# Q and K of three token groups by seven block products instead of eight, and the sums of W1 and W2 on another queue

## The chip, the cores and the metric

The kernel runs on one core of one Trainium2 chip. The core has TensorE (matrix products, results in PSUM), VectorE and ScalarE (elementwise work, both read PSUM), GpSimd (elementwise work, SBUF only) and SyncE, which issues most of the transfers. Each engine takes its own instructions in order. PSUM has eight banks of 128 x 512 float32. The metric is the device time of one execution in microseconds; the lower the better. Given is the median of three runs.

## The reference

One transformer block with conditioning, in float32, for 2 rows of 2048 tokens of width 512, 16 heads of 32, hidden width 2048:

```python
mod = silu(condition) @ Wada + bada              # 6 parts of width 512 for each row
sh_a, sc_a, gt_a, sh_m, sc_m, gt_m = split(mod, 6, axis=1)
xn = layernorm(x, g1, be1)
xm = xn * (1 + sc_a) + sh_a
x = x + gt_a * attention(xm, Wqkv, Wproj, bproj)  # causal, softmax over keys
xn = layernorm(x, g2, be2)
xm = xn * (1 + sc_m) + sh_m
h = gelu(xm @ W1 + b1)
x = x + gt_m * (h @ W2 + b2)
```

## The kernel before

For each of the two rows the kernel runs a Q, K, V stage (`Qkv.run`), an attention stage (`attention_phase`) and a projection (`project_phase`); after the second row comes a feed-forward stage for all tokens.

**The Q, K, V stage** takes the row's tokens in four groups g of 512 (`MT`). A group has 12 units n: eight for Q and K, in the order Q and K of output chunk f = 0, then of f = 1 to 3 (a chunk is 128 outputs, four heads), and four for V, one for each 128 tokens. A unit of Q or K is four products of a 128 x 128 block of `Wqkv` with 512 normalized, transposed tokens (`xmT`), added up in one PSUM bank (`ps_qk`, tag "mm", six banks in turn). A float32 product is two TensorE instructions. ScalarE then copies the bank to the first half of a tile `hl`, rounded to float32r (L860), VectorE subtracts that from the bank for the second half (L861), and SyncE stores the tile (L866). There are four `hl` tiles. This pair of ScalarE and VectorE steps is called the split below.

**Hooks.** After unit n, `between(n)` runs what belongs to other things: loads of the next tokens, their statistics, their normalization (n = 5, 8), their transposes through PSUM and the modulation that writes the next `xmT` (n = 6, 9; half of it by VectorE at L286, half by ScalarE at L291, unless `by_act`). It also calls `also(g, n)`, see below. After each product, `among(n, k)` may add attention scores of the same row: one score (`Row.score`, `Row.bank`) is a product of 128 queries with up to 512 keys into one of two banks with the tag "s", of which VectorE takes the maximum of each row (L484, or L479 where the causal mask cuts in). The number of scores at each place is worked out when the program is written, so that in group 1 the first of the attention units (4 heads by 512 queries) is scored and in groups 2 and 3 the next two. The keys and queries for that are loaded back from memory by SyncE (L339, L348) after chunk 0 of the group is stored.

**Sums of W1 and W2.** The feed-forward stage multiplies blocks two by two by the Strassen-Winograd scheme, with seven products and not eight; it needs sums of the blocks of W1 and W2, which are prepared during the Q, K, V stages. `Quarters` does this in 16 parts: `load` brings four blocks (L955, four transfers of 128 KB), `make` forms four sums on GpSimd (L967) and stores the seven blocks (L970, 896 KB). `FirstLayer` does a second level for W1 in the Q, K, V stage of row 1 (L997, L992, L1021). All of these transfers are issued by GpSimd. `also` calls them at fixed units; with at = 12 g + n, row 0 has 13 of the 16 parts, one each four units until at = 29 (`free`) and one each two units after that.

**Order.** Instructions wrapped in `act` or `mm` keep their program order on their engine; the others are ordered by a planner when the program is built, by its own model of time. Waits between engines are put in from the data that each instruction reads and writes.

**Memory reused.** `vv` holds the values of the row's 16 token tiles; tiles of tag "x" hold incoming tokens; four tiles "qst" hold the queries of attention units; `bgate` and `fold` are used in attention and projection.

Of the kernel before, what the change touches and what calls it, by code (L numbers as in the profile page):

```python
# [8 lines left out]
F32 = mybir.dt.float32  # L9
# [8 lines left out]
P = 128  # L18
# [9 lines left out]
def dit_block_kernel(  # L28
# [765 lines left out]

    class Qkv:
# [35 lines left out]
        def norm(self, g, j):  # L831

            b = self.row.b
            if j == 0:
# [3 lines left out]
                self.xmT[g][:, :, j * 2 * P : (j + 1) * 2 * P],  # L838
            )

        def group(self, g, hp, between, among):
# [5 lines left out]
            n = 0  # L847
            for f in range(C):
                for which in range(2):
                    ps = psum.tile([P, MT], F32, tag="mm", name="ps_qk")  # L850
                    w0 = which * D + f * P
                    for k in range(C):
                        mm(
                            ps, w[:, k, w0 : w0 + P], xmT[:, k, :],
                            start=(k == 0), stop=(k == C - 1),
                        )
                        among(n, k)
                    hl = hp.tile([P, 2, MT], F32R, tag="hl", name="hl", bufs=4)
                    scale = HD**-0.5 if which == 0 else 1.0
                    nc.scalar.activation(hl[:, 0, :], ps, AF.Copy, scale=scale)  # L860
                    nc.vector.scalar_tensor_tensor(  # L861
                        hl[:, 1, :], ps, scale, hl[:, 0, :].bitcast(F32),
                        ALU.mult, ALU.subtract,
                    )
                    dst = (qd if which == 0 else kd)[b][f]
                    nc.sync.dma_start(  # L866
                        dst[:, :, tok].rearrange("l p t -> p l t"), hl.bitcast(F32)
                    )
                    between(n)
                    n += 1  # L870
                if f == 0:
                    row.load_keys(0, g)
                    row.load_queries(g)
            for t in range(MTT):
# [9 lines left out]
                n += 1  # L884

        def run(self, hp, also):

            row = self.row
            for g in range(NG):

                def between(n):
                    if g + 1 < NG:
# [8 lines left out]
                        if n == 9 and g + 2 < NG:  # L901
                            self.load_x(g + 2)
                    elif n == 8:

                        row.rows(0)
                        act(nc.scalar.activation(first, eps, AF.Exp))
# [27 lines left out]
    class Quarters:  # L934
# [6 lines left out]
        def __init__(self):  # L941
            self.at, self.loaded = 0, []
# [1026 lines left out]
```

## Time and profile before

| | |
|---|---|
| median of 3 runs | 2307.22 us (2301.46 to 2310.62) |
| the profiled execution | 2301.71 us, its span on the core 2300.0 us |
| granted TensorE clock, mean | 0.999 |
| Q, K, V stage of row 0, groups 0 to 3 | 44.7, 47.6, 54.8, 49.7 us |
| Q, K, V stage of row 1, groups 0 to 3 | 43.0, 45.5, 51.9, 49.6 us |

The times of the groups are the lengths between the first products of Q and K of each, taken from the timeline of TensorE. In the rows of the profile, "PE" is TensorE's products, "PEld" its weight loads, "DVE" VectorE, "ACT" ScalarE, "POOL" GpSimd, "SP" SyncE. A row names the line of the kernel, the operation and "out<-in" by the names of the tiles; "<-" behind an idle time names who ended it. L204 is the helper through which every matrix product goes, so products are told apart by their tiles. The end of a matrix product is modelled and takes in the way through the array: products that follow each other overlap in their rows, and their pace is read from the starts.

### The profile page before, as it was taken

What the parts mean: (1) busy time and instruction counts of PE and PEld (TensorE: products, weight loads), DVE (VectorE), ACT (ScalarE), POOL (GpSimd) and SP (SyncE); (2) the same over time, 40 slices, a digit from 0 to 9 for tenths busy, and PEclk for the clock granted to TensorE, in tenths of its full rate; (3) what the DMA queues carried; (4) which work ended last, traced back from release to release, by engine and by line L of the source; (5) the groups of instructions that cost most, each with busy time, mean ns of one, the idle gap of its engine ahead of it and who ended that gap; (6) DMA issues with size and microseconds to landing.
All of it is one profiled execution on the core that took longest, in us unless ns stands there. A gap on an engine that the chain in (4) does not pass through costs nothing. (4 is left out here: it accounts for less than half of the span.)

```text
span 2300.0 us, 33469 instructions
## 1 busy us (share of the span) xinstructions
PE 2257.8 (98%) x12141; PEld 1384.9 (60%) x12141; DVE 1547.8 (67%) x3088; ACT 946.0 (41%) x1808; POOL 1291.1 (56%) x1036
## 2 busy tenths in 40 slices
PE   8999999999999999999999999999999999999998
PEld 3455455555554445554455545446888888888887
DVE  3366776777765525677677777555896876877787
ACT  2222555555556122155555555632332242252230
POOL 3335887878884543248788787553764602602510
PEclk9999999999999999999999999999999999999999
DMA  9867405151142799651421404265375654654643
GB/s 311 273 199 238 108 24 122 46 120 47 37 149 96 245 315 333 234 133 29 102 60 38 111 24 134 86 224 198 121 268 209 208 176 158 201 183 150 211 146 115
DMA packets 118525, 355.60 MB, mean 155 GB/s; under 512 B 14497, under 2 KB 15053, under 8 KB 103641
## 3 DMA queue, kind: packets, MB, share of 16 engines
q1 hardware_dynamic: 107040, 293.64, 42.0%
q0 software_dynamic: 10944, 59.28, 7.2%
q8 instruction: 96, 1.57, 0.3%
q14 instruction: 69, 0.56, 0.1%
q10 hardware_dynamic: 376, 0.55, 0.1%
HBM read 253.80 MB, written 107.48 MB: 157 GB/s over the span
## 5 line engine op out<-in xcount | busy, mean ns | idle before, releaser
L619 ACT ACTIVATE e<-st 128x512 f32<-128x512 f32 (+1 forms) x1152 | 573.4, 579 | 396.4 <-PE st L204 353.7
L484 DVE TENSOR_REDUCE mx<-s 128x1 f32<-128x512 f32 x612 | 413.3, 687 | 190.6 <-PE s L204 189.4
L649 POOL TENSOR_TENSOR ee<-ee,e 128x1024 f32<-128x1024 f32 x212 | 498.5, 2382 | 7.7 <-ACT e L619 7.7
L204 PE MATMUL s<-kst,qst 128*128 128x512 f32 (+3 forms) x1032 | 473.2, 460 | 11.9 <-DVE mx L484 5.8
L204 PE MATMUL st<-qst,kst 128*128 128x512 f32 (+3 forms) x1280 | 400.9, 378 | 0.0
L204 PE MATMUL ps_a<-sum,room 128*128 128x256 f32 x1504 | 356.8, 381 | 4.5 <-DVE c L1452 1.5
L204 PEld LDWEIGHTS ps_a<-sum,room 128*128 128x128 f32 x1504 | 281.2, 190 | 54.3 <-issue 6.0
L204 PE MATMUL o<-e,vv 128*32 128x512 f32 (+3 forms) x2560 | 300.8, 538 | 0.9 <-POOL e L628 0.9
L479 DVE CUSTOM_DVE_ANT_0 junk<-s,causal 128x128 bf16<-128x128 f32 (+3 forms) x420 | 206.0, 491 | 120.8 <-PE s L204 112.9
L204 PEld LDWEIGHTS s<-kst,qst 128*128 128x128 f32 x1032 | 193.9, 188 | 143.2 <-issue 65.1
L204 PEld LDWEIGHTS st<-qst,kst 128*128 128x128 f32 x1280 | 229.0, 188 | 68.2 <-issue 39.1
L649 POOL TENSOR_TENSOR ee<-e 128x1024 f32<-128x1024 f32 x84 | 198.2, 2382 | 118.6 <-ACT e L619 118.5
L204 PE MATMUL ps_qk<-xmT,wqkv 128*128 128x512 f32 x512 | 240.7, 598 | 1.8 <-DVE xmT L286 1.8
L628 POOL TENSOR_SCALAR_AFFINE_SELECT e<-e 128x256 f32<-128x256 f32 x256 | 103.7, 435 | 131.4 <-ACT e L619 129.4
L204 PEld LDWEIGHTS ps_qk<-xmT,wqkv 128*128 128x128 f32 x512 | 94.5, 191 | 98.4 <-issue 91.5
L1680 POOL TENSOR_TENSOR c<-c,h 128x512 f32<-128x512 f32 x40 | 58.6, 1484 | 159.1 <-ACT c L1678 159.1
L204 PEld LDWEIGHTS <-sel 32*128 32x128 bf16 x1152 | 29.7, 91 | 192.0 <-issue 189.9
L204 PE MATMUL ps_b<-sum,room 128*128 128x256 f32 x608 | 143.6, 379 | 0.0
L204 PEld LDWEIGHTS ps_b<-sum,room 128*128 128x128 f32 x608 | 115.0, 190 | 15.4
L204 PE MATMUL ps_v<-wqkv,xmT 128*128 128x512 f32 x256 | 122.1, 594 | 0.0
L204 PE MATMUL st<-fold,sel 32*128 32x512 bf16 (+1 forms) x1152 | 117.9, 372 | 4.3 <-DVE mhl L505 2.8
L204 PEld LDWEIGHTS o<-e,vv 128*32 128x32 f32 x2560 | 61.5, 108 | 98.7 <-issue 80.2
(182 smaller groups left out, 2945.8 us busy)
## 6 DMA issues: line engine op xcount, KB each, us to landing
qst<-q SPq DMA_DIRECT2D x128, 256.0 KB
room<-w1e SPq DMA_DIRECT2D x28, 1024.0 KB
kst<-k SPq DMA_DIRECT2D x24, 1024.0 KB
room<-w1e SPq DMA_DIRECT2D x28, 768.0 KB
room<-w2e SPq DMA_DIRECT2D x21, 1024.0 KB
q<-hl SPq DMA_DIRECT2D x32, 512.0 KB
k<-hl SPq DMA_DIRECT2D x32, 512.0 KB
room<-w2e SPq DMA_DIRECT2D x21, 768.0 KB
```

What stands on the lines that cost most here:

```text
L204: return tc.keep_in_program_order(nc.tensor.matmul(*args, **kw))
L479: nc.vector.tensor_tensor_reduce(junk[:, :w], s[:, :w], causal[:, QB - w :], 1.0, MASKED, ALU.add, ALU.max, m,)
L484: nc.vector.tensor_reduce(m, s[:, :w], axis=AX.X, op=ALU.max)
L619: act(nc.scalar.activation(e[:, h % 2, :w], sts[h][:, :w], AF.Exp))
L628: nc.gpsimd.affine_select(d, d, pattern=[[0, 2], [1, P]], compare_op=ALU.is_ge, fill=0.0, base=0, channel_multiplier=-1,)
L649: act(engine.tensor_tensor(dst, x, y, ALU.add))
L1680: nc.gpsimd.tensor_tensor(c, c, piece_of(base, i, t, pair), ALU.add)
```

## The change

Group 0 of each row stays as it was. In groups 1 to 3, Q and K go by pairs of output chunks (f = 0, 1 and f = 2, 3). For one pair, the outputs are split in two chunks, the 512 inputs in two halves and the 512 tokens in two halves, and the 2 x 2 by 2 x 2 block product is formed by seven block products (`sevens`). A block product is two matmuls of 128 x 128 weights with 256 tokens. Q and K of a pair run as two sets in turn: one product for Q, one for K, and so on. A set uses two PSUM banks, w and u, one for each output chunk; partial results are copied out by ScalarE to `kept` tiles (three a set) and added back by VectorE (three sums a set). Then each bank goes through the same split as before (`keep`).

The sums that this needs are formed by GpSimd: three new weight blocks for each set and one in place, after units 4 and 8 of group 0 (`weight_sums`), kept in an unused "qst" tile, `fold` and `bgate` (`scratch`); and four token blocks for each coming group at unit 10 (`token_sums`), kept in parts of `vv` that aren't filled yet, one new tile and tiles of tag "x". A group now begins with two units of V, then come the two pairs (units 2 to 5 and 6 to 9), then two units of V. Keys and queries are loaded after the first pair, not after chunk 0. The first "qst" tile is scratch, so the load of the fourth unit's queries waits until group 3 has used the weight sums in it.

The modulation of all groups but the very first is now wholly ScalarE's (`by_act`).

The transfers of `Quarters` and `FirstLayer` are issued by SyncE, and the store is a step of its own, called later than the sums. In row 0 the loads come at at = 11, 15, ..., 27, then 29, 31, ..., 43, the sums one unit after, the stores one unit after the sums (two where the loads come each two units); in row 1 `FirstLayer` loads at 11, 15, 22, 26, 35, 39, 43, sums two units later and stores four later.

```diff
@@ Qkv.norm
+                by_act=b > 0 or g > 0,
@@ Qkv.group
+            if g == 0:
...
+            n, half = 2 * C, MTT // 2
+            for t in range(half):
+                values(t, t)
+            for pair in range(C // 2):
+                self.sevens(g, pair, half + pair * C, keep, between, among)
+                if pair == 0:
+                    asked()
+            for t in range(half, MTT):
+                values(t, n + t)
+        def weight_sums(self, which, pair):
+            a = self.blocks(which, pair)
+            s1, s2, s4 = self.s[which, pair]
+            for d, x, y, op in (
+                (s1, a(1, 0), a(1, 1), ALU.add),
+                (s2, s1, a(0, 0), ALU.subtract),
+                (s4, a(0, 1), s2, ALU.subtract),
+                (a(1, 0), a(0, 0), a(1, 0), ALU.subtract),
+            ):
+                act(nc.gpsimd.tensor_tensor(d, x, y, op))
...
+            for d, u, v in (
+                (t1, x(0, 1), x(0, 0)),
+                (t2, x(1, 1), t1),
+                (t3, x(1, 1), x(0, 1)),
+                (t4, x(1, 0), t2),
+            ):
+                act(nc.gpsimd.tensor_tensor(d, u, v, ALU.subtract))
+        def sevens(self, g, pair, n, keep, between, among):
...
+            w = [self.psum.tile([P, MT], F32, tag="mm", name="ps_w") for _ in both]
+            u = [self.psum.tile([P, MT], F32, tag="mm", name="ps_u") for _ in both]
+            def product(ps, m, v, new=False):
+                for kk in range(2):
+                    mm(
+                        ps, m[:, kk, :], v[:, kk, :],
+                        start=new and kk == 0, stop=kk == 1, skip_group_check=not new,
+                    )
+                at = len(done)
+                done.append(n + at * 8 // 7 // 4)
+                among(done[-1], at * 8 // 7 % 4)
...
+            for q in both:
+                then = product(u[q][:, lo], a[q](0, 0), x(0, 0), True)
+                copy(kept[q][0], u[q][:, lo])
+                then()
+            for q in both:
+                then = product(w[q][:, hi], s[q][0], t1, True)
+                copy(kept[q][1], w[q][:, hi])
+                then()
+            for q in both:
+                then = product(u[q][:, lo], s[q][1], t2)
+                copy(kept[q][2], u[q][:, lo])
+                then()
+            for q in both:
+                then = product(w[q][:, hi], s[q][2], x(1, 1))
+                total(w[q][:, hi], w[q][:, hi], kept[q][2])
+                then()
+            for q in both:
+                then = product(u[q][:, lo], a[q](1, 0), t3)
+                total(u[q][:, hi], u[q][:, lo], kept[q][1])
+                then()
+            for q in both:
+                then = product(w[q][:, lo], a[q](0, 1), x(1, 0))
+                total(w[q][:, lo], w[q][:, lo], kept[q][0])
+                keep(w[q], q, 2 * pair)
+                then()
+            for q in both:
+                then = product(u[q][:, lo], a[q](1, 1), t4)
+                keep(u[q], q, 2 * pair + 1)
+                then()
@@ Qkv.run, between(n)
+                        if g == 0 and n == 4:
+                            self.scratch()
+                        if g == 0 and n in (4, 8):
+                            for which in range(2):
+                                self.weight_sums(which, n // 8)
+                        if n == 10:
+                            self.token_sums(g + 1)
@@ Quarters.load, .make, .store
-                act(nc.gpsimd.dma_start(w[:, n], src))
+                act(nc.sync.dma_start(w[:, n], src))
...
+        def store(self):
+            f, w = self.made.pop(0)
             dst = (w1d if f < FC // 2 else w2d)[:, :, :, f % (FC // 2), :]
             act(
-                nc.gpsimd.dma_start(
+                nc.sync.dma_start(
@@ row 0, also(g, n)
-            if 9 <= at < free:
-                if at % 4 == 1:
+            if 11 <= at <= free:
+                if at % 4 == 3:
                     quarters.load(room[0])
-                elif at % 4 == 3:
+                elif at % 4 == 0:
                     quarters.make()
-            elif at >= free and at % 2 == 1:
+                elif at % 4 == 1 and quarters.made:
+                    quarters.store()
+            if at >= free:
...
+                if at % 2 == 1 and quarters.at < early:
                     quarters.load(room[quarters.at % 2])
+                elif at % 2 == 0:
+                    if quarters.made:
+                        quarters.store()
+                    if quarters.loaded:
+                        quarters.make()
```

158 lines of the change are left out of this document (111 added, 47 removed).

## The prediction

> **What bounds the kernel now.** I read the page first: the engine shares, then the costliest groups.
>
> ```profile
> PE 2257.8 (98%) x12141; PEld 1384.9 (60%) x12141; DVE 1547.8 (67%) x3088; ACT 946.0 (41%) x1808; POOL 1291.1 (56%) x1036
> ...
> L204 PE MATMUL ps_a<-sum,room 128*128 128x256 f32 x1504 | 356.8, 381 | 4.5 <-DVE c L1452 1.5
> L204 PEld LDWEIGHTS ps_a<-sum,room 128*128 128x128 f32 x1504 | 281.2, 190 | 54.3 <-issue 6.0
> ...
> L204 PE MATMUL ps_qk<-xmT,wqkv 128*128 128x512 f32 x512 | 240.7, 598 | 1.8 <-DVE xmT L286 1.8
> ```
>
> TensorE is busy 98% of the span, and before its 512 instructions for Q and K it stood idle 1.8 us in all. So work taken off TensorE there is time, until another engine binds. A share is a mean, so next comes the table of busy times over the stretches of the three later token groups of row 0 and of row 1. Its columns are the stretch, its length, then busy time of TensorE, weight loads, VectorE, ScalarE and GpSimd, the granted clock, the DMA share and GB/s.
>
> ```profile
> 65.10:112.70 47.60, 47.60 (x146) 22.66 (x145) 20.06 (x61) 13.62 (x26) 13.41 (x18) 1.00 0.93 296
> 112.70:167.50 54.80, 54.16 (x178) 28.01 (x177) 34.35 (x90) 12.98 (x25) 21.22 (x31) 1.00 0.68 205
> 167.50:217.20 49.70, 49.70 (x141) 24.78 (x140) 30.32 (x64) 8.38 (x14) 24.92 (x37) 1.00 0.80 243
> ...
> 842.20:887.70 45.50, 45.50 (x129) 22.31 (x128) 19.58 (x59) 12.92 (x25) 18.32 (x18) 1.00 1.01 352
> 887.70:939.60 51.90, 51.26 (x155) 26.82 (x154) 33.00 (x85) 13.11 (x26) 23.89 (x23) 1.00 0.99 349
> 939.60:989.20 49.60, 49.60 (x137) 24.73 (x135) 30.29 (x64) 8.37 (x14) 0.00 (x0) 1.00 0.45 138
> ```
>
> TensorE fills each stretch at full clock. But VectorE is at 61 to 64% in groups 2 and 3 (30.32 of 49.70): they carry the attention scores beside Q and K. And the DMA engines are at 0.68 to 1.01 in all but the last. These are the two covers that the change leans on.
>
> **The change on TensorE.** One matmul of the program is two instructions here. Their spacing is read from unbroken runs in the timeline (start, duration, count); a row's own duration holds the drain too and can't be used.
>
> ```profile
> 799.25 24.20 PE L204 MATMUL ps_qk<-xmT,wqkv 128*128 128x512 f32 x56
> 823.29 1.04 PE L212 MATMUL ps_xt<-ident,x 128*128 128x128 f32 x8
> ...
> 2004.93 1.89 PE L204 MATMUL ps_b<-xm,room 128*128 128x256 f32 x8
> ...
> 2013.57 0.81 PE L204 MATMUL ps_a<-sum,room 128*128 128x256 f32 x3
> ```
>
> (823.29 - 799.25) / 56 = 0.429 us for 512 columns; (2013.57 - 2004.93) / 40 = 0.216 us for 256, in the feed-forward stage, which already multiplies by sevens. A pair (two output chunks of Q and of K) is 4 x 4 matmuls of 512 now, 32 instructions, 13.73 us; after, 2 sets x 7 products x 2 matmuls of 256, 56 instructions, 12.10 us. That is 1.63 us less; two pairs in three groups of two rows are 12 pairs: **19.6 us less**. The 24 added weight loads of a pair cost nothing of their own as long as each hides under a stream of 0.216.
>
> In the feed-forward rows it does: eight weight loads of 0.19 fit in each 1.73 us. If loads didn't overlap, a pair would go from 32 x 0.619 to 56 x 0.406 us, 2.9 longer, and the kernel to 2307 + 35 = 2342. The Trainium skill (TensorE: Matmul & The Clock Gate, "The mechanism") says that a weight load overlaps with matmuls in flight only where their row groups differ, which is that case, since all these use all rows; the spacing of 0.216 with 0.19 loads speaks against it here.
>
> **What waits inside a set of seven.** Each product needs the copy or sum made of its bank by ScalarE or VectorE before. With two sets in turn, three other products, 3 x 0.86 = 2.6 us, lie between. A copy or a sum takes about 0.4:
>
> ```profile
> L1452 DVE TENSOR_TENSOR c<-y,ps_a x40: 406/420/422, 1689.8 to 2281.7; 128x256 f32<-128x256 f32 x40
> L1768 ACT COPY c<-ps_a x16: 372/372/377, 1663.9 to 2221.3; 128x256 f32<-128x256 f32 x16
> ```
>
> In the feed-forward stage, with one set at a time, all 1504 instructions of the first group on the page waited 4.5 us together. I take 0 for this chain as such. ScalarE gains 72 copies of 0.372, and by_act moves 4 modulations each of seven group preparations to it; at 8 to 14 us of 45 to 55 it has room.
>
> **VectorE in groups 2 and 3** is the dear term. A set adds three sums of 0.42; 72 in all, 30 us; by_act takes off 28 modulations of 0.53, 15 us, but none in group 3, which prepares no next group. The rows of groups 2 and 3 of row 0, by shape:
>
> ```profile
> L484 DVE TENSOR_REDUCE mx<-s 128x1 f32<-128x512 f32 x48 | 33.0, 688 | 18.6 <-PE s L204 18.5
> L861 DVE SCALAR_TENSOR_TENSOR hl<-ps_qk,hl 128x512 fp32r<-128x512 f32 x16 | 11.0, 685 | 14.4 <-ACT hl L860 14.4
> ...
> L286 DVE TENSOR_SCALAR xmT<-ps_xt,a,c 128x256 f32<-128x256 f32 x4 | 2.0, 534 | 0.0
> ```
>
> The work isn't spread evenly: the splits (L861) of a pair all fall on its last four products. There VectorE has 2 sums of 0.42, 4 splits of 0.69 and 4 scores of about 0.65 (an estimate: two of three are the first row's 0.69, masked ones are shorter): 6.2 us. TensorE has 4 products of 0.864 and 4 scores of 0.21 ((49.70 - 48 x 0.858) / 41): 4.3 us. VectorE falls 1.9 us behind, and TensorE feels it through the two score banks:
>
> ```profile
> 955.22 0.69 DVE L484 TENSOR_REDUCE mx<-s 128x1 f32<-128x512 f32 x1 [0.40 <-PE s L204]
> 955.83 0.68 DVE L861 SCALAR_TENSOR_TENSOR hl<-ps_qk,hl 128x512 fp32r<-128x512 f32 x1
> ...
> 960.50 0.69 DVE L484 TENSOR_REDUCE mx<-s 128x1 f32<-128x512 f32 x1
> ```
>
> ```profile
> 959.66 0.80 PE L204 MATMUL s<-kst,qst 128*128 128x512 f32 x1
> ```
>
> The score started at 959.66 is reduced at 961.19, 1.53 us later, and its bank is wanted two products on, after 2.15: 0.6 us of slack. So 1.9 - 0.6 = 1.3 us of stall; rows that follow directly start 0.61 and not 0.69 apart, which over ten rows gives 0.8 back: 0.5. I take 1.0 for each of the 8 pairs of groups 2 and 3, since the split of a sum also has to wait for ScalarE's 0.60: **8 us more**. Ends: 0 (the scores order themselves around it), and 2.5 a pair, 20 us, if VectorE idles 0.6 before both splits that follow a sum. Group 1 has 16 scores on its 40 slots, not 40, and I take 0.
>
> **GpSimd** gains 32 weight sums of 0.74 and 24 token sums of 1.27 us, and loses its DMA issues:
>
> ```profile
> L992 POOL TENSOR_TENSOR w<-w 128x512 f32<-128x512 f32 x28 | 35.0, 1272 | 2.0 <-DMA w<-w1d 1.3
> L967 POOL TENSOR_TENSOR w<-w 128x256 f32<-128x256 f32 x12 | 8.5, 742 | 8.6 <-DMA w<-in_L_cond_W_dram 8.4
> L955 POOL DMA_DIRECT2D w<-in_L_cond_W_dram x12 | 6.4, 546 | 5.6 <-DMA w2d<-w 3.6 <-DMA w<-w1d 1.9
> ```
>
> At 13 to 25 us of 45 to 55 it has room. Token sums start at unit 10; the first is wanted after three units of V (10.3 us) and two products, 12 us later; modulation and sum take 3.5. Cost 0; without the cover the price is the 5.1 us of four sums a group.
>
> **SyncE** takes over the loads and stores of W1 and W2, in order with the stores of Q and K and the loads of keys and queries. What is queued behind a waiting load there is the store of a split, and behind that, with four hl tiles, ScalarE's next split. From unit 33 to 43 of row 0, six loads each wait for a store issued one unit before.
>
> ```profile
> L970 POOL DMA_DIRECT2D w1d<-w x8: 1067/1067/1109, 23.7 to 167.5; - x8
> ...
> DMA to landing us min/median/max: 5.4/5.8/11.3
> ```
>
> A cycle is landing 5.8, four issues of 0.55 and the store, 8.6 us, for two units of TensorE at (49.70 - 3.3 + 2) / 12 = 4.0 each, 8.1. SyncE falls 0.5 x 6 = 3 us behind; an hl tile is reused a pair, 15 us, later and needs 5.8 to land, so 9 are covered: cost 0. Already now the splits of units 6 and 7 of group 3, whose products end near 196 and 200 (units of 4.1 from 167.5), come at 206.32, and TensorE is busy all through that stretch, which supports the cover:
>
> ```profile
> 206.32 1.06 ACT L860 ACTIVATE hl<-ps_qk 128x512 fp32r<-128x512 f32 x2
> ```
>
> **The start.** GpSimd's first load of W1 now shares the DMA engines with the load that TensorE needs:
>
> ```profile
> 5.37 2.90 POOL L955 DMA_DIRECT2D w<-in_L_cond_W_dram  x4
> ...
> 14.97 1.72 PE L204 MATMUL ps_mod<-wada,sc 128*32 128x512 f32 x4 [0.23 <-DMA wada<-in_L_cond_Wada_dram]
> ```
>
> It goes to unit 11. 0.5 MB at about 300 GB/s is 1.7 us, the most that this can give; 0 the least. I take 0.8 less.
>
> **The sum.** -19.6 - 0.8 + 8.0 = -12.4 us. The profiled execution took 2301.7 us (span 2300.0) and is 5.5 under the median of three, so it would go to 2289; against the median of 2307.2 I predict **2295 us**.
>
> **Rivals.**
> 1. VectorE keeps up, no stall: 2307 - 21 = 2286. For it: it is 61 to 64% busy over a group. Against it: the four products above.
> 2. VectorE becomes the bound at every pair's end: with 2.5 us a pair the gain of groups 2 and 3 is gone, 2307 - 20.4 + 20 = 2307. For it: L861 already idles 14.4 us for ScalarE's half.
> 3. Slower: SyncE's queue. With stores landing in 11.3 us, as the slowest did, a cycle is 14.1, six cycles fall 36 us behind, 9 covered: a stall of 27 in row 0, 2307 - 12 + 27 = 2322. It eats the gain from a lag of 9 + 12 = 21 us on, that is landings over 8.8 us on average. For it: DMA shares near 1. Against it: the median of 5.8.
> 4. Weight loads that don't hide: 2342, as worked out above. Against it stand 1504 rows of this kernel.
>
> **How the numbers follow.** Forecast (stalls of 4 to 13 us, 2290 to 2299) 0.52, rival 1 0.15, rival 2 0.17, rival 3 0.15, rival 4 0.01. A change under 0.5%, 11.5 us, is about what measurement can't tell from none. Faster by more (under 2295.7): rival 1's 0.15 and somewhat over half of the forecast, 0.30, make 0.45; within: the other 0.22 of it and rival 2's 0.17, 0.39; slower: rivals 3 and 4, 0.16. The range for 8 in 10 runs from just under rival 1 to past rival 2 and into rival 3, 2284 to 2315.
>
> **What would show it.** Right: rows of 128x256 spaced 0.216 for Q and K; group 1 stretches down by 3.3 us (47.6 to 44.3), groups 2 and 3 by 1 to 1.5; TensorE's idle for VectorE before scores up from under 1 us to about 8; first Q product about 1 us earlier than 20.37. Wrong: stretches of groups 2 and 3 as long as before (rival 2), or ScalarE's splits waiting on stores of hl and TensorE idle behind them in units 38 to 48 of row 0 (rival 3), or Q and K rows spaced over 0.25 (rival 4).

## The result, and the profile after

The changed kernel takes 2318.4 us (median of six runs, 2315.4 to 2320.6); the kernel before took 2304.0 beside it (six runs). The ratio is 1.0059, with a 95% interval of 1.0042 to 1.0077: 10 to 18 us slower, where I had predicted 12 us faster. The profiled execution took 2319.8 us (span 2318.1).

The page of the changed kernel, engine shares and packets:

```profile
PE 2248.9 (97%) x12429; PEld 1443.0 (62%) x12429; DVE 1560.1 (67%) x3132; ACT 981.8 (42%) x1908; POOL 1279.0 (55%) x998
...
DMA packets 153858, 355.66 MB, mean 153 GB/s; under 512 B 14496, under 2 KB 56012, under 8 KB 138968
```

TensorE is 9 us less busy than before (2248.9 against 2257.8), though the kernel is longer: part of the gain shows even so, and waits have eaten it. The stretches of groups 1 to 3 of row 0, then of row 1, for the changed kernel. They run from the first product of a group's first pair to that of the next group's, so that each holds eight units of Q and K and four of V, as before. The one of group 3 is carried 6.9 us past the attention's first score, for the two units of V that this group now has ahead of its first pair: its length compares with the one before, but the busy times in its last 6.9 us are the attention's. Columns as in the prediction.

```profile
68.47:112.69 44.22, 44.22 (x193) 31.71 (x192) 21.93 (x68) 18.13 (x41) 7.21 (x11) 1.00 0.91 264
112.69:180.42 67.73, 53.53 (x226) 37.71 (x225) 37.25 (x100) 18.43 (x41) 25.33 (x30) 0.92 0.81 234
180.42:229.70 49.28, 47.12 (x202) 34.30 (x201) 38.69 (x89) 16.15 (x33) 14.97 (x23) 1.00 0.89 263
854.96:897.70 42.74, 42.40 (x177) 31.35 (x176) 20.91 (x67) 18.27 (x41) 15.01 (x12) 1.00 0.86 281
897.70:952.94 55.24, 51.19 (x203) 36.51 (x202) 36.50 (x95) 18.64 (x41) 18.23 (x15) 0.97 0.86 303
952.94:1002.30 49.36, 44.52 (x184) 32.23 (x183) 36.73 (x84) 13.36 (x27) 12.10 (x11) 1.00 0.80 268
```

Group 1 is shorter by 3.4 and 2.8 us (47.60 and 45.50 before), group 3 by 0.4 and 0.2. Group 2 is longer, by 12.9 us in row 0 (54.80 before) and 3.3 in row 1 (51.90). What TensorE waited for in the whole of the changed kernel, and then in the kernel before (total, times, longest):

```profile
PE s L204 <- DMA qst<-q: 11.5, 1, 11.5
PE s L204 <- DVE mx L484: 9.3, 12, 1.4
...
PE s L204 <- DVE mhl L505: 5.8, 11, 1.1
PE st L204 <- ACT e L619: 4.3, 2, 4.1
...
PE s L204 <- DVE mx L479: 2.9, 4, 1.5
```

```profile
PE s L204 <- DVE mx L484: 5.8, 10, 0.8
PE s L204 <- DVE mhl L505: 4.7, 10, 0.6
```

Two single waits are new. **In group 2 of row 0** TensorE stands 11.5 us before the first score of the third attention unit, because that unit's queries aren't there (for the first 1.5 us of this the score has to wait for VectorE anyway, whose last step for the unit before ends at 154.1). SyncE's queue from the end of the first pair on (start, duration, line, transfer):

```profile
130.67 0.37 SPq L861 DMA_DIRECT2D q<-hl  x1
131.22 0.62 SPq L1136 DMA_DIRECT2D w1d<-w  x1
134.49 0.37 SPq L861 DMA_DIRECT2D k<-hl  x1
135.09 0.77 SPq L861 DMA_DIRECT2D q<-hl  x1
137.98 1.94 SPq L1116 DMA_DIRECT2D w<-in_L_cond_W_dram  x4
140.02 0.41 SPq L861 DMA_DIRECT2D k<-hl  x1
140.48 0.48 SPq L339 DMA_DIRECT2D kst<-k  x1
145.25 0.53 SPq L1136 DMA_DIRECT2D w1d<-w  x1
145.87 3.85 SPq L1116 DMA_DIRECT2D w<-in_L_cond_W_dram  x4
149.76 1.42 SPq L339 DMA_DIRECT2D kst<-k  x3
151.22 2.70 SPq L348 DMA_DIRECT2D qst<-q  x4
```

The last K of the pair (VectorE ended its split at 135.66), the three later loads of keys and all loads of queries stand behind a load of W1 that waits for a store to land (137.98), a store that waits for GpSimd's sums (145.25) and the next load. The last load of queries is issued at 153.9. They land at about 164, as TensorE's row shows:

```profile
164.05 1.19 PE L204 MATMUL s<-kst,qst 128*128 128x512 f32 x2 [11.47 <-DMA qst<-q]
165.04 1.91 PE L204 MATMUL ps_v<-wqkv,xmT 128*128 128x512 f32 x2
```

Stretches of these microseconds, columns as above:

```profile
158.00:162.00 4.00, 0.00 (x0) 0.00 (x0) 0.00 (x0) 0.00 (x0) 0.00 (x0) 0.50 1.11 205
162.00:164.00 2.00, 0.00 (x0) 0.00 (x0) 0.00 (x0) 0.00 (x0) 0.00 (x0) 0.50 1.16 274
164.00:166.00 2.00, 1.95 (x5) 1.27 (x5) 1.15 (x2) 0.00 (x0) 0.81 (x2) 0.50 1.10 360
166.00:168.00 2.00, 2.00 (x6) 0.97 (x4) 0.44 (x3) 0.00 (x0) 1.92 (x3) 0.64 1.13 374
```

The DMA engines are full (share over 1) and move only 205 to 274 GB/s while TensorE waits. The clock granted to it fell to 0.50 at about 157.2 and was full again at about 167.4: 3.4 us of work at half the clock, so that the stall costs an estimated 1.7 us more than its length.

**At the start of row 1's attention** the exponentials wait for a store. Their tiles take the room of FirstLayer's tiles, whose last store is called at unit 47. SyncE, ScalarE and TensorE there:

```profile
994.64 0.33 SPq L1190 DMA_DIRECT2D w1e<-w  x1
...
1003.12 1.09 ACT L619 ACTIVATE e<-st 128x512 f32<-128x512 f32 x2 [4.78 <-DMA w1e<-w]
1003.76 1.07 PE L204 MATMUL st<-fold,sel 32*128 32x512 bf16 x2 [4.14 <-ACT e L619]
```

The granted clock is 0.50 from about 1003.7 to 1013.9, and the first product with the values comes 17.0 us after the first score, where it took 9.5 before.

The account by stages, after less before in us: first Q product -1.8, row 0's group 0 -1.7, groups 1 -6.1, groups 2 +16.3, groups 3 -0.7, the two attention starts +0.6 and +7.5, the rest of the attention +0.4, the feed-forward stage +3.5: together +18 of one profile against the other. Two of these terms aren't the change's. The feed-forward stage, from its first product with a tile `sum`, took 720.9 us before and 724.4 after, but 720.6 to 725.6 in the executions below, and 724.5 in one of the kernel before with one edit far from it. And the -1.7 in row 0's group 0 is the clock: the profile of the kernel before has 0.50 granted there from about 20.8 to 24.3 us, that of the changed kernel has 1.00 throughout. Of the other 16 runs with seven products, 9 have such a low clock there, with 51.6 us from the first Q product to the first pair, and 7 haven't, with 49.9. Without the two, +16 remains.

### The profile page after: what moved, and what is told of

It reads as the page before. It is cut to its first block, busy times and chain, and to the rows that moved or that the text cites. A ratio compares the mean times of both kernels' runs of the same rounds, so it can differ in the third digit from the quotient of the medians.

```text
span 2318.1 us, 34368 instructions
## 1 busy us (share of the span) xinstructions
PE 2248.9 (97%) x12429; PEld 1443.0 (62%) x12429; DVE 1560.1 (67%) x3132; ACT 981.8 (42%) x1908; POOL 1279.0 (55%) x998
## 2 busy tenths in 40 slices
DMA packets 153858, 355.66 MB, mean 153 GB/s; under 512 B 14496, under 2 KB 56012, under 8 KB 138968
## 5 line engine op out<-in xcount | busy, mean ns | idle before, releaser
L484 DVE TENSOR_REDUCE mx<-s 128x1 f32<-128x512 f32 x612 | 413.3, 687 | 225.3 <-PE s L204 223.8
L204 PE MATMUL s<-kst,qst 128*128 128x512 f32 (+3 forms) x1032 | 438.1, 427 | 30.6 <-DMA qst<-q 11.5
L628 POOL TENSOR_SCALAR_AFFINE_SELECT e<-e 128x256 f32<-128x256 f32 x256 | 104.4, 441 | 84.9 <-ACT e L619 51.9
L1128 POOL TENSOR_TENSOR w<-w 128x256 f32<-128x256 f32 x64 | 45.2, 729 | 142.0 <-DMA w<-in_L_cond_W_dram 130.2
L484 DVE TENSOR_REDUCE mx<-st 128x1 f32<-128x512 f32 x156 | 107.0, 686 | 3.8 <-PE st L204 1.3
```

The costliest lines, as they stand in the source:

```text
L204: return tc.keep_in_program_order(nc.tensor.matmul(*args, **kw))
L484: nc.vector.tensor_reduce(m, s[:, :w], axis=AX.X, op=ALU.max)
L628: nc.gpsimd.affine_select(d, d, pattern=[[0, 2], [1, P]], compare_op=ALU.is_ge, fill=0.0, base=0, channel_multiplier=-1,)
L1128: act(nc.gpsimd.tensor_tensor(w[:, n], w[:, x], w[:, y], op))
```

## The experiments

My theory (A) was that SyncE's queue makes the loss: the queries and keys of group 2 and the last store of FirstLayer. The rival (B) was that the seven products don't pay in groups 2 and 3, since VectorE binds. Ratios are to the kernel before, run beside each, with 95% intervals.

### The two halves apart

Seven products, with the transfers of W1 and W2 on GpSimd and called as in the kernel before:

```diff
-                act(nc.sync.dma_start(w[:, n], src))
+                act(nc.gpsimd.dma_start(w[:, n], src))
...
-            if 11 <= at <= free:
-                if at % 4 == 3:
+            if 9 <= at < free:
+                if at % 4 == 1:
                     quarters.load(room[0])
```

> The changed kernel with all transfers of Quarters and FirstLayer back on GpSimd and at the units of the kernel before; Q and K by seven products stay. Theory A (SyncE's queue made the loss: the queries of group 2 come 11.5 us late in row 0, and the last store of sums stands ahead of the attention of row 1 for 7.5 us): both stalls go, with them the low clock behind the first (some 2 us): 2318 - 11.5 - 2 - 7.5 = 2297, group 2 of row 0 down from 67.7 to about 54. Theory B (the sevens themselves don't pay in groups 2 and 3, since VectorE binds there): group 2 stays above 60 us, and the time stays at 2310 or over. What would speak for neither: TensorE waiting for the token sums, which now stand behind GpSimd's loads.

Eight products, with these transfers on SyncE and called as in the changed kernel:

```diff
-                act(nc.gpsimd.dma_start(w[:, n], src))
+                act(nc.sync.dma_start(w[:, n], src))
```

> The kernel before with only the transfers of Quarters and FirstLayer moved to SyncE, at the units of the changed kernel; Q and K by eight products, and keys and queries asked for after unit 1 of a group. Theory A: the queries of group 2 are asked for four units before the loads come each two units, so that stall is small, but the attention of row 1 still starts 7.5 us late: 2304 + 7.5 - 1.8 (start) = 2310, up to 2320 if the queries are late here too. Theory B: no loss from the queue, 2302 to 2304.

Both were wide of both theories: 1.0159 (1.0140 to 1.0178) and 1.0159 (1.0144 to 1.0174), some 37 us slower each, while both together cost 14. TensorE's waits with seven products and GpSimd's queue:

```profile
PE s L204 <- DMA qst<-q: 13.4, 2, 7.4
...
PE o L204 <- POOL e L628: 7.1, 3, 6.2
...
PE ps_w L204 <- POOL vv L959: 5.8, 2, 4.0
```

On GpSimd, loads that wait for a store to land stand ahead of the token sums that the sevens need (L959) and of the masks of the attention (L628). So, with the calls where the kernel before has them, that queue doesn't serve the sevens. With eight products and SyncE's queue, ScalarE and SyncE at the start of row 1's attention:

```profile
1007.32 12.01 SPq L1029 DMA_DIRECT2D w1e<-w  x2
```

```profile
1025.98 1.08 ACT L619 ACTIVATE e<-st 128x512 f32<-128x512 f32 x2 [13.01 <-DMA w1e<-w]
```

SyncE is so far behind that two stores of FirstLayer are left at 1007. The move to SyncE with the new call times, which I had priced at nothing, costs 37 us when done alone. First products with the values come 19.2 and 24.5 us after the first scores (8.9 and 9.5 before), and row 1's group 2 takes 60.6 us (51.9 before).

### Asked late, or queued?

In the changed kernel keys and queries are also asked for four units later. That alone, in the kernel before:

```diff
-                if f == 0:
+                if f == (0 if g == 0 else 2):
                     row.load_keys(0, g)
```

> The kernel before with one edit: keys and queries of groups 1 to 3 are asked for after unit 5 of their group, as in the changed kernel, and not after unit 1. All transfers of W1 and W2 stay on GpSimd. Theory A1 (the stall before the scores of group 2 comes of the late asking itself, four units later on DMA engines that are busy): TensorE waits 5 to 10 us before these scores, 2301 + 8 = 2309. Theory A2 (it comes of SyncE's queue, that is of the loads and stores that stand ahead there): under 2 us, 2301 to 2303.

1.0004 (0.9990 to 1.0018): no cost. SyncE's rows there, with group 2 starting at 114.27:

```profile
144.48 1.86 SPq L348 DMA_DIRECT2D qst<-q  x3
```

The last query load is issued 32 us after the pair's first product, and nothing waits. But this doesn't clear the late asking in the changed kernel: here VectorE ends the unit before only 46.3 us after that product, so that the queries are wanted later than there (41.4). The next run takes the loads of keys and queries out of SyncE's queue:

```diff
@@ Row.load_keys
-                nc.sync.dma_start(
+                (nc.gpsimd if c == 0 and g > 0 else nc.sync).dma_start(
@@ Row.load_queries
-                nc.sync.dma_start(
+                (nc.gpsimd if 0 < u < NQ else nc.sync).dma_start(
```

> The changed kernel with the loads of keys and queries of groups 1 to 3 issued by GpSimd in place of SyncE. Theory A: they no longer stand behind the loads and stores of W1 in SyncE's queue, and the 11.5 us that TensorE waits for queries in group 2 of row 0 go, with some 2 us of low clock: 2318 - 13 = 2305. Theory B (the keys and queries are late because the stores of Q and K land late, or because the DMA engines are full): the wait stays at 8 us or more, 2315 to 2318.

1.0028 (1.0019 to 1.0038), 2307.8 us. TensorE's wait in group 2 of row 0 falls from 11.5 to 2.2 us, the stretch is 56.4 us in place of 67.7. GpSimd's queue there, with the pair starting at 114.87, and TensorE:

```profile
141.24 1.09 POOL L348 DMA_DIRECT2D qst<-q  x2
142.32 2.18 POOL L339 DMA_DIRECT2D kst<-k  x4
144.50 1.09 POOL L348 DMA_DIRECT2D qst<-q  x2
```

```profile
156.51 0.70 PE L204 MATMUL s<-kst,qst 128*128 128x512 f32 x2 [2.22 <-DVE mhl L505]
```

VectorE's step L505 ends at 155.8 and the last query load lands at 156.3, so that 0.7 us of the 2.2 are still the queries'. The issue is 10.5 us earlier than in the changed kernel, and from its end to the score it's about 11 us here and 10 there: the DMA engines didn't get faster, the queue let go earlier. Theory A holds for this stall. Which of SyncE's work stands in the way? First the stores alone were taken off it, and called at the end of `make`:

```diff
             self.made.append((f, w))
+            self.store()
...
-                nc.sync.dma_start(
+                nc.gpsimd.dma_start(
                     dst.rearrange("p n c d -> p (n c) d"),
```

> The changed kernel, with the stores of the sums (Quarters and FirstLayer) issued by GpSimd right behind its sums; the loads stay on SyncE at the same units. Theory A1 (SyncE's queue is held by stores that wait for GpSimd's sums): the 11.5 us wait for the queries of group 2 shrinks to under 5, the last store of FirstLayer falls at unit 45 and not 47, so that the wait at the start of row 1's attention loses some 4 us: 2318 - 7 - 2 - 4 = 2305. Theory A2 (the queue is held by loads that wait for the store ahead of them to land, and by full DMA engines): the loads still wait, the queries still come 8 us or more late, 2314 to 2318.

1.0047 (1.0032 to 1.0061); the wait stays at 11.0 us, A2. Then row 0's loads were moved so that none comes at units 28 to 32, the later ones to 33, 35, ..., 43:

```diff
-            if 11 <= at <= free:
-                if at % 4 == 3:
-                    quarters.load(room[0])
+            if at in (8, 11, 14, 17, 20, 23, 26):
+                quarters.load(room[0])
...
-                if at % 2 == 1 and quarters.at < early:
+                if at % 2 == 1 and at >= 33 and quarters.at < early:
```

> The changed kernel with one edit: row 0's parts of W1 and W2 are loaded at units 8, 11, 14, 17, 20, 23, 26 and then 33, 35, ..., 43, so that SyncE's queue and the DMA engines have no loads of W1 between unit 28 and unit 33, where the keys and queries of group 2 are asked for. Theory B1 (the queries are late because loads of W1, ahead of them in the queue and beside them on full DMA engines, come in these units): the 11.5 us wait goes, with 2 us of low clock: 2318 - 13 = 2305. Theory B2 (they are late because VectorE finishes the splits of the first pair late and their stores take long to land, whatever else is loaded): the wait stays at 6 us or more, 2312 to 2318.

1.0118 (1.0102 to 1.0133), slower still, and no test of the pause: in group 1 the queue fell behind. Its loads of W1 there, with the same room each time:

```profile
78.67 2.50 SPq L1116 DMA_DIRECT2D w<-in_L_cond_W_dram  x4
91.05 2.03 SPq L1116 DMA_DIRECT2D w<-in_L_cond_W_dram  x4
104.44 4.21 SPq L1116 DMA_DIRECT2D w<-in_L_cond_W_dram  x4
123.66 1.91 SPq L1116 DMA_DIRECT2D w<-in_L_cond_W_dram  x4
```

```profile
132.42 2.08 PE L204 MATMUL ps_w<-vv,qst 128*128 128x256 f32 x4 [9.31 <-POOL vv L959]
```

One room goes round in 12 to 19 us: load, landing, sums, store, landing. GpSimd's weight sums wait for those loads, and the token sums wait behind them. The pause came again with group 1 left at its pace, and two parts moved to row 1:

```diff
-        free, early = 2 * (C * 2 + MTT) + 5, 13
+        free, early = 2 * (C * 2 + MTT) + 5, 11
-                if at % 2 == 1 and quarters.at < early:
+                if at % 2 == 1 and at >= 33 and quarters.at < early:
...
-            late_loads = (11, 15, 22, 26, 35, 39, 43)
+            late_loads = (11, 20, 24, 28, 32, 36, 40)
```

> The changed kernel with 11 parts in row 0 (loads at units 11, 15, 19, 23, 27, 33, 35, ..., 43) and five in row 1 (units 0, 1, 6, 7, 12), FirstLayer's loads then at 11, 20, 24, 28, 32, 36, 40. Group 1 keeps its pace of one part each four units, unlike the run with the pause, and no load of W1 is called at units 28 to 32. Theory B1 (loads of W1 ahead of the keys and queries and beside them): the wait for queries in group 2 of row 0 falls from 11.5 to under 3 and the low clock goes, -11; the last store at unit 44 takes some 4 off the attention of row 1: 2318 - 15 = 2303. Theory B2 (splits and stores of the first pair alone make it late): the wait stays over 7, 2310 to 2314.

1.0048 (1.0029 to 1.0067). The wait shrinks to 7.8 us in row 0, and one of 4.5 appears in row 1:

```profile
159.87 1.19 PE L204 MATMUL s<-kst,qst 128*128 128x512 f32 x2 [7.78 <-DMA qst<-q]
```

Nearer to B2: the loads at 28 to 32 are a part of it, not the whole. The runs together show what counts. For row 0's group 2, from the timelines, counted from the first pair's first product: the end of the last query load's issue; the end of VectorE's last step for the unit before, for which the first score has to wait too; the start of that score; and TensorE's wait ahead of it.

| kernel | issued, us | VectorE ready, us | first score, us | wait, us |
|---|---|---|---|---|
| before | 14.7 | 47.6 | 48.0 | 0 |
| asked on GpSimd | 30.7 | 40.9 | 41.6 | 2.2 |
| before, asked late | 32.1 | 46.3 | 46.8 | 0 |
| asked on GpSimd, FirstLayer earlier (below) | 33.6 | 43.0 | 44.4 | 3.0 |
| the same, and stores on GpSimd (below) | 35.9 | 40.3 | 47.9 | 9.2 |
| two parts in row 1 | 38.0 | 41.0 | 47.3 | 7.8 |
| seven products, all on GpSimd | 40.6 | 45.6 | 50.1 | 6.0 |
| changed kernel | 41.2 | 41.4 | 51.4 | 11.5 |
| stores on GpSimd | 42.2 | 42.1 | 51.6 | 11.0 |
| pause | 51.6 | 54.0 | 59.9 | 7.5 |

Wherever TensorE waits in this table, the first score starts 8 to 12 us after the last issue. Keys and queries of a group are 2 MB (8 loads of 256 KB), which at 205 to 274 GB/s is an estimated 8 to 10 us by itself. With VectorE ready after 41 us, the cover of the changed kernel ends at an issue some 31 us after the pair's first product. Its row 1 is just inside: issued at 29.9, first score at 40.7, 0.05 us after VectorE's step. In row 0, 41.2 came together from a pair that is complete only at its end, and from about 9 us of queueing (140.48 to 149.76).

### VectorE

The third unit's scores were moved into group 3, where the queries have time:

```diff
-                            past += 40 * (g - 2)
-                            row.score(
-                                row.count(
-                                    cum[0] + (cum[2] - cum[0]) * past / 80,
-                                    1 if g == 2 and n < 7 else 2,
-                                )
-                            )
+                            was, to = cum[g - 2], cum[g - 1]
+                            row.score(row.count(was + (to - was) * past / 40, g - 1))
```

> The changed kernel, but the third attention unit's scores all fall in group 3: 32 scores on the 40 products of group 2, 48 on those of group 3, in place of 40 and 40. The keys and queries of group 2 are then wanted some 20 us later. Theory A (they come late, and TensorE stands before their first score): the 11.5 us and 2 us of low clock behind them go, group 2 of row 0 from 67.7 to 54 or less, and group 3 grows by its eight scores of 0.21, 1.7 us, less what group 2 sheds: 2318 - 13 = 2305. Theory B (VectorE is so near its bound that eight more scores in group 3 cost it eight times 0.65): group 3 grows to 55, and the time stays at 2311.

1.0029 (1.0014 to 1.0043), 2309.4 us, between the two: groups 2 fall to 50.9 and 49.0 us, groups 3 rise to 54.7 and 52.8, as B had it. But 5 us more were lost where neither theory looked: the first product with the values comes 13.0 us after the first score in row 0, and 19.0 in row 1. With VectorE's share of the modulations given back:

```diff
-                by_act=b > 0 or g > 0,
```

> As the run with the scores moved to group 3, with the modulations shared by ScalarE and VectorE again, as in the kernel before. VectorE gets 28 modulations of 0.53 back, 8 of them in each row's groups 1 and 2 in which group 2 and group 3 are prepared. If VectorE binds in group 2, those of group 2 show at full price in both rows, 2 x 4 x 0.53 = 4 us, and 2305 becomes 2309; if it has room there, as I took for all but the last four products of a pair, 2305 stays within 1.5.

1.0036 (1.0023 to 1.0049), not to be told from the run without it: the medians, 2309.4 and 2310.3 us, are 1 us apart, and the spread of the ten executions of each leaves room for some 3, less than the 4 of a full price. So VectorE isn't full over a group. And, in the changed kernel as it stands, the statistics moved off the first pair:

```diff
-                        if 1 <= n <= MTT and g >= row.b:
-                            self.stats(g + 1, n - 1, True)
+                        if g >= row.b and g == 0:
+                            if 1 <= n <= MTT:
+                                self.stats(g + 1, n - 1, True)
+                        elif n < 2 and g > 0:
+                            self.stats(g + 1, 2 * n, True)
+                            self.stats(g + 1, 2 * n + 1, True)
```

> The changed kernel with one edit: the statistics of the next group's tokens (four a group, 0.68 us of VectorE each) are called in groups 1 and 2 after units 0 and 1, the two units of values, and not after units 1 to 4, beside the first pair. Theory B1: VectorE's backlog in the first pair falls by some 2 us, the scores' waits for VectorE there shrink by 2 to 3 us in each row, but the queries stay late: 2318 - 4 = 2314. Theory B2: the splits of the first pair end 2 us sooner and the queries with them: 2318 - 4 - 3 = 2311, the wait for queries down to 8.

1.0045 (1.0029 to 1.0062), not to be told from the changed kernel. Groups 2 took 68.0 and 56.1 us, the wait for queries 12.8. Neither B1's nor B2's gain is in the stretches.

### The start of row 1's attention

FirstLayer's loads come earlier, and with them its last store:

```diff
-            late_loads = (11, 15, 22, 26, 35, 39, 43)
+            late_loads = (11, 15, 19, 23, 27, 31, 35)
```

> The changed kernel with FirstLayer's seven loads in row 1 at units 11, 15, 19, 23, 27, 31, 35, so that its last store falls at unit 39 and not at 47. Theory A: the exponentials of row 1's attention no longer wait for the room of the last store; the 7.5 us between its first score and its first product with the values go: 2318 - 7.5 = 2311. Row 0 stays as it is. Theory B (the start of the attention waits for something else, or the transfers in a denser row stall group 2): 2318 or more.

1.0092 (1.0075 to 1.0109). The mechanism was right, and the time went elsewhere: the first product with the values comes 8.7 us after the first score in place of 17.0, but in row 1 the queries of group 2 are late by 7.3 us and token sums by 4.1, and the stretch of group 2 goes from 55.2 to 67.5. With more room between the loads, and with the edit that moves the scores to group 3:

```diff
-            late_loads = (11, 15, 22, 26, 35, 39, 43)
+            late_loads = (11, 15, 20, 25, 30, 34, 38)
```

> As the run with the scores moved to group 3, and FirstLayer's loads at units 11, 15, 20, 25, 30, 34, 38, so that its last store is called at unit 42 and not at 47. Theory A: row 1's attention starts its products with the values 8 us sooner, as where the loads came at 11 to 35, and without the price that those had in group 2 (keys and queries late by 7 us), since the queries now have time: 2305 - 8 = 2297, faster than the kernel before by 4 to 6. Theory B (a denser queue in row 1 puts its price elsewhere, on the token sums that GpSimd makes behind its weight sums): some 4 us before the first products of groups 2 and 3, 2301 to 2305.

1.0007 (0.9990 to 1.0023), 2302.0 us: as fast as the kernel before, not faster. Row 1 is right now (9.8 us at the attention's start). Row 0 isn't: group 3 takes 57.0 us, and the attention starts 3 us late. GpSimd there:

```profile
223.69 2.90 POOL L1123 TENSOR_TENSOR w<-w 128x256 f32<-128x256 f32 x4 [14.41 <-DMA w<-in_L_cond_W_dram]
226.54 2.92 POOL L628 TENSOR_SCALAR_AFFINE_SELECT e<-e 128x256 f32<-128x256 f32 x8
```

The attention's first masks stand behind the last weight sums, and these behind a load. In no run does row 0's first product with the values come before 225.3 us; in the kernel before it comes at 226.1. In the four runs above that took the wait for queries in group 2 away (all but 0.7 us in one) and left row 0's loads and stores as they are on SyncE's queue it comes at 225.3 to 227.2, 11.6 to 13.0 us behind the first score (8.9 before): what TensorE saves ahead of it is handed back there.

### Together

Four more runs had the stores on GpSimd or keys and queries on GpSimd, with FirstLayer's loads at 11, 15, 20, 25, 30, 34, 38.

> As the run with the stores on GpSimd, and FirstLayer's loads at units 11, 15, 20, 25, 30, 34, 38. Theory A1: both stalls of SyncE's queue are gone; what stays over the time before is VectorE's (some 7 us more waits of scores in groups 2) against 19.6 + 1.8 gained: 2302 - 21 + 10 = 2291. Theory A2: row 0's stall stays, 2314 - 8 = 2306.

1.0022 (1.0009 to 1.0034). A2: the wait in row 0 stays, 9.2 us; row 1 is clean (42.3, 52.9 and 49.3 us, then 8.9), 3 us shorter than before from its first Q product to its first product with the values.

> As the run with stores on GpSimd and the loads of FirstLayer moved, with the third attention unit's scores in group 3 alone. Theory A1: nothing waits for queries either way, VectorE has 5 us less in groups 2 and 5 us more in groups 3, where TensorE stood 5 us more in row 0 when this was tried with the stores on SyncE: 2291 to 2295. Theory A2: the scores' move takes the stall of row 0 away and the rest of the queue's lateness stays at the start of row 0's attention (4 us): 2302 - 3 = 2299.

1.0006 (0.9989 to 1.0023), 2306.3 us, with 15.2 us at the start of row 0's attention: A2's place, though its 2299 wasn't reached. 4.3 us of that start are one more wait for queries, those of the fourth unit, issued at 210.2 and used at 219.8.

> As the run with stores on GpSimd and the loads of FirstLayer moved, with keys and queries of groups 1 to 3 asked for on GpSimd too, so that SyncE's queue has the loads of W1 and W2 and the stores of Q and K. Theory A1: as without it, 2291, or 2 to 4 more if the keys' loads hold GpSimd's sums back while they wait for the stores of K. Theory A2 (the loads on SyncE hold back the queries): this one is the fast one, 2307.8 - 8 = 2300 or below, and the run without it stays 5 us above it.

1.0024 (1.0008 to 1.0040). Neither: with keys and queries behind GpSimd's sums and stores, the last of them is issued 35.9 us after the pair's start and the wait of 9.2 is back.

> The changed kernel with keys and queries of groups 1 to 3 asked for on GpSimd, and FirstLayer's loads at units 11, 15, 20, 25, 30, 34, 38; the stores of sums stay on SyncE. With the first edit alone it took 2308, with the second the start of row 1's attention lost 7 to 8 us elsewhere. If the two stalls are separate, 2308 - 8 = 2300, 0.1% under the kernel before; if the second comes back as a wait for queries or token sums in row 1, 2304 to 2308.

1.0017 (1.0005 to 1.0030), the second case. Row 1's attention starts in 9.5 us, but its group 2 takes 63.8 (54.7 with the first edit alone), with waits of 3.6 and 2.9 us and a low clock behind each (0.66 on average from 900 to 905 us, 0.53 from 940 to 945). GpSimd's last query loads there, and TensorE:

```profile
920.06 1.63 POOL L348 DMA_DIRECT2D qst<-q  x3
```

```profile
938.72 1.19 PE L204 MATMUL s<-kst,qst 128*128 128x512 f32 x2 [2.94 <-DMA qst<-q]
```

They take 17 us to land, beside FirstLayer's loads and stores, with the DMA engines' share at 1.00 to 1.03 from 920 to 940: they are issued already, so no queue of an engine holds them.

Last, the pause of units 28 to 32 with the stores on GpSimd, and with the statistics moved as well:

> Row 0's parts loaded with the pause at units 28 to 32, stores of sums on GpSimd, FirstLayer's loads at units 11, 15, 20, 25, 30, 34, 38. Without the pause this was 2307. Theory B1: the wait of 9 us before the scores of group 2 and the low clock behind it go: 2307 - 11 = 2296, below the kernel before by 6. Theory B2: 2303 to 2307.

> As the run before this one, with the statistics in the units of values too. If VectorE's backlog in the first pairs of groups 2 is what is left of the loss there (52.9 us in row 1 where TensorE's own work is 48.5 by the 51.9 of before less 3.3), it takes 2 to 3 us off each row: 2296 - 5 = 2291. If the last products of a pair carry it, as I had it, under 2 us in all: 2295.

1.0084 (1.0069 to 1.0099) and 1.0079 (1.0064 to 1.0094): the crowded group 1 again, with token sums late by 13.0 and 14.9 us in all.

## Why the prediction was wrong

It said 2295 us (2284 to 2315), and it is 2318. By its own steps:

1. **TensorE, -19.6: right.** Group 1, where little else competes, lost 3.4 and 2.8 us against 3.3. That also answers rival 4: the added weight loads hide. The Trainium skill (TensorE: Matmul & The Clock Gate, "The mechanism") has one sentence by which weight loads overlap with matmuls in flight only where row groups differ, and these all use all of them; but another of the same section also lets a load into the background weight buffer go ahead. These stretches speak against the first alone and agree with the second.
2. **The chain inside a set, 0: right** in group 1.
3. **VectorE, +8: right in kind, too small.** Waits of scores for VectorE went from 10.5 to 18.0 us. Group 3 gained 0.4 and 0.2 where TensorE saves 3.3, so 1.5 a pair is lost and not 1.0. Row 1's group 2, in a run where no queries were late there (the first of the last group), lost 52.9 - (51.9 - 3.3) = 4.3, 2.1 a pair, 2.9 of it as waits for VectorE. If row 0's group 2 is like it, that is 15 us in all, inside the ends of 0 and 20. That VectorE takes all of it isn't shown: the recorded waits grew by 7.5 us, and neither the modulations nor the statistics showed a price that would say where in a pair it is lost.
4. **GpSimd, 0: right here, with a thin cover.** Wherever the loads ran late, GpSimd's weight sums held back the token sums, up to 10.6 us at one place.
5. **SyncE, 0: the step that failed.** The prediction said that "what is queued behind a waiting load there is the store of a split". It never priced the loads of keys and queries queued there, though the text of the change says that they move from chunk 0 to the first pair, nor the last store of FirstLayer ahead of row 1's attention. Its cycle of 8.6 us was for units 33 to 43, where two rooms take turns, and there the loads did come 7.0 to 9.6 us apart (168.90 to 200.96). What it left out is the queue before that. With one room, load, landing, sums, store and landing follow one another, with stores and loads of Q and K between them, and the loads up to unit 27 came 14.1, 19.6, 21.1 and 16.8 us apart; the last of them, at 137.98, stood ahead of the keys and queries. With the queue 3 us behind by its sum, the last load of row 0, called at unit 43 (about 205 us: six units of 4.1 after 180.4), was issued at 220.6, some 15 us late. Together 11.5 for the queries, 2 for the clock behind them and 7.5 at row 1's attention make 21 us that stood at 0.
6. **The start, -0.8:** -1.8, past the 1.7 given as the most; 1.2 to 2.4 in the runs with seven products and SyncE's queue, and 2.4 with GpSimd's, where the first load of W1 also came later (at 47.4).

With 7 more for VectorE and 21 for SyncE, less 1 at the start, -12 becomes +15: within the interval of +10 to +18.

Rival 3 had the engine, the sign and nearly the time (2322), by another way: it had stores of hl land late and ScalarE's splits wait. No split waited for a store in the changed kernel. The price was paid by the readers of that queue, not by the writers, so that 2322 came near 2318 by chance.

**Still open:** what the 8 to 12 us from issue to score would be on freer DMA engines. In row 0 taking the keys and queries off SyncE's queue took the wait from 11.5 to 2.2 us by an earlier issue alone; in one run row 1 was late on the engines alone. That a schedule exists which keeps TensorE's 20 us wasn't shown: the two best versions here are level with the kernel before.

## What to carry to other kernels

When transfers move to another engine's queue, list everything that this queue issues afterwards and who waits for it: loads with a deadline stand behind stores that wait for another engine, and the deadline is where the price shows, not the transfer. Work out the cycle of a reused room as the whole round (issue, landing, compute, store, landing). And where a stage's end hangs on a chain of transfers that already ran to its end, time saved on TensorE ahead of it comes back as a wait there.

## What I had not expected of the hardware

A store or load that waits at the head of SyncE's queue holds up issues behind it for which everything is ready (the store of the last K from 135.66 to 140.02, the loads of keys from 140.48 to 149.76 above). The Trainium skill (DMA: Bandwidth & Descriptors, "Issuing engines are not separate DMA queues") says that issuing from several engines only saves the time to initiate the DMA; here asking on GpSimd in place of SyncE took TensorE's wait from 11.5 to 2.2 us, since the loads no longer stood behind others, while the 17 us of landing with keys and queries on GpSimd and FirstLayer earlier agree that the engines behind are shared.

Full DMA engines moved very different amounts: at shares over 1, 205 GB/s while keys and queries landed, and 374 GB/s a few microseconds later. The queue also changes the packets: 56012 of under 2 KB with the transfers of W1 and W2 on SyncE, by sevens or by eights, and 15052 by sevens with all of these on GpSimd (15053 in the kernel before).

TensorE's stall of 11.5 us had its granted clock at 0.50 from 4.6 us after its start to 3.4 us after work began. The Trainium skill (TensorE: Matmul & The Clock Gate, "What's actually happening") gives the same two states and about 3.4 us for each change; by that rule work after such a stall runs at half clock for 3.4 us, an estimated loss of 1.7 us, and this stall agrees. The wait of 4.1 us at the start of row 1's attention doesn't: there the clock stayed at 0.50 for some 10 us after work began (1003.7 to 1013.9), though TensorE's rows fill that time. Why isn't known.
